# Layer 0 of a four-layer graph network: the destinations' one-hot compared with places held in PSUM

## The chip, the core and the metric

The kernel runs on one core of a Trainium2 chip. Its time is the device time of one launch in microseconds (us); smaller is better. The core's engines run unsynchronized and hand work to each other through semaphores: TensorE (PE, with its weight loads as PEld), VectorE (DVE), ScalarE (ACT), GpSimd (POOL) and SyncE (SP). Here POOL issues the indirect gathers and SP the plain DMAs.

## The reference, cut to what matters

Four layers follow each other on 6250 nodes and 100,000 edges, sorted by destination. The change is in layer 0, an attention over each node's incoming edges:

```
alpha = leaky_relu(s[src] + s[dst], 0.2)        # per edge and head
m     = segment_max(alpha, dst)
e     = exp(alpha - m[dst])
a     = e / segment_sum(e, dst)[dst]
attn  = segment_sum(Vh[src] * a, dst)           # then a projection, norms and a feed-forward
```

The edges also carry a loop from every node to itself. For each edge, `s[dst]` and the subtracted maximum have to be fetched from the destination's row, and the weighted values have to be added into the destination's row. The kernel does both with matrices of zeros and ones.

## The kernel before

**Groups.** The edges are cut into G = 98 groups of 1024 (8 columns j of 128 edges). Because the edges are sorted, a group's destinations lie in a window of 128 nodes that begins at 64*g - 32. A node block of 128 rows is put together from the windows that overlap it.

**The layer-0 edge loop** (from L812 on, under a schedule written out by hand: every engine keeps exactly the order of the source) runs once for each group g:

- POOL issues eight gathers of source rows into one of six buffers (`rows0`, L130; tile `xbuf`). A buffer may be filled again only when the sums of the group six before it are done.
- SP loads the group's destination numbers, spread over all partitions (`drow`, L742), two groups ahead, into three buffers.
- `logits0` (L771, L123, L773 on DVE) makes `al`, the exponent; ACT takes its exponential twice: into PSUM as `ex` (tile `ps_E`, L774) and into the gathered rows (L775).
- `one_hot_t` (L748 on DVE) makes `to` for the **next** group: for each edge, in the transposed layout, a one in the partition whose node is the edge's destination. It compares `drow` (int32) with a per-partition number, column g of `place`.
- L836 on DVE multiplies the gathered values by `ex`, in place.
- `of_dst` (L763 on PE) multiplies `to` of the next group with the score table, into one of two PSUM buffers `ps_A`. The next group's logits read it.
- `sum_window` (L681 on PE) sums the group's rows into `ps_S` with a second one-hot, `oh` (L754 on DVE, made a group ahead); ACT copies the sum out as `ws` (L691).
- Every second group also closes a node block: L699 (`ps_T`, shifted sums of the windows), L781 to L786 (division), L792 and L800 (turn and project), L808 and L810 (residual and statistics).

On ACT the order is: both exponentials of g, `ws` of g, in every second group the copy L794, then the exponentials of g + 1. On DVE it is: `al` of g, `to` of g + 1, the product L836 of g, then the rest. On PE it is: shifted sums or projection, `of_dst` of g + 1, the sum of g.

PSUM has eight buffers here, of which the tag "E" is one; it is taken anew for each group by `ps("E", ...)`.

Of the kernel before, what the change touches and what calls it, by code (L numbers as in the profile page):

```python
# [13 lines left out]
OP = mybir.AluOpType  # L14
# [3 lines left out]
P = 128  # L18
J = 8
W = 128  # L20
D = 256
H = 8
# [13 lines left out]
def tile_gnn(ctx: ExitStack, tc: tile.TileContext, a: dict, out: bass.AP, N: int):  # L36
# [11 lines left out]
    nc = tc.nc  # L48
# [3 lines left out]
    G = GJ // J  # L52
# [69 lines left out]
    def leaky(o, y, slope):  # L122
        nc.vector.scalar_tensor_tensor(o, y, slope, y, op0=OP.mult, op1=OP.max)  # L123
# [76 lines left out]
    with ExitStack() as l0:  # L200
        wp = l0.enter_context(tc.tile_pool(name="w0", bufs=1))
        ps = l0.enter_context(Psum("psa", T=2, Q=2, V=2, X=2))
# [453 lines left out]
    def fast():  # L656
        wp = fctx.enter_context(tc.tile_pool(name="wl", bufs=1))
        psc = fctx.enter_context(ExitStack())
        ps = psc.enter_context(Psum("ps0", S=2, A=2, T=1, B=2, E=1))
# [57 lines left out]
        with tc.tile_pool(name="e0", bufs=2) as ep:  # L717

            scw = ep.tile([P, NB, 2, 2 * H], F32, name="scw", bufs=1)
            for odd in range(2):  # L720
                for b0, b1 in ((0, 32), (32, NB)):
# [6 lines left out]
                    else:  # L728
# [5 lines left out]
            place = ep.tile([P, G], F32, name="place", bufs=1)  # L734
            nc.gpsimd.iota(place, pattern=[[HW, G]], base=-OFF, channel_multiplier=1,
                           allow_small_or_imprecise_dtypes=True)
            sums, drows, tos, dgs, ohs, mades, vs, ms, mts = {}, {}, {}, {}, {}, {}, {}, {}, {}

            def loads0(g):
# [4 lines left out]
            def one_hot_t(g):  # L744

                if g < G:
                    tos[g] = ep.tile([P, J * P], F32, name="to")
                    nc.vector.tensor_scalar(tos[g], drows[g], place[:, g:g + 1], None, OP.is_equal)  # L748

            def one_hot0(g):  # L750
                if g < G:
# [14 lines left out]
            def logits0(g):  # L766

                vg, dg = vrows[g % NV], dgs[g]
                al = ep.tile([P, J, H], F32, name="al")
                ex = ps("E", [P, J, H])  # L770
                nc.vector.tensor_tensor(al, vg[:, :, D:D + H], dg[:, :, 0:H], OP.add)  # L771
                leaky(al, al, 0.2)
                nc.vector.tensor_tensor(al, al, dg[:, :, H:2 * H], OP.subtract)  # L773
                nc.scalar.activation(ex, al, AF.Exp)  # L774
                nc.scalar.activation(vg[:, :, D:D + H], al, AF.Exp)  # L775
                return ex
# [35 lines left out]
            with tc.manual_schedule():  # L812
                for g in range(2):
                    loads0(g)
                one_hot_t(0)
                one_hot0(0)
                of_dst(0)
                for g in range(G + 2):
                    vg = vrows[g % NV]
                    if AHEAD <= g < G:  # L820
                        rows0(g)
                    loads0(g + 2)
                    for b in blocks_done(g):
                        vs[b] = ep.tile([P, H, HD], F32, name="v")
                        nc.sync.dma_start(vs[b], vt[b * P:(b + 1) * P, 0:D].rearrange("p (h c) -> p h c", c=HD))
                    if g == 6:
                        made(of1)
                    if g == 8:
                        made(of2)
                    summed = [(b, sum_block(sums, b, VR)) for b in blocks_done(g - 1)]  # L830
                    projected = [(b, project0(b)) for b in blocks_done(g - 2)]
                    if g < G:
                        ex = logits0(g)
                        one_hot_t(g + 1)
                        vals = vg[:, :, 0:D].rearrange("p j (h c) -> p j h c", c=HD)
                        made_g = nc.vector.tensor_tensor(  # L836
                            vals, vals, ex[:, :, :, None].to_broadcast([P, J, H, HD]), OP.mult)
                    of_dst(g + 1)
                    for b, s in summed:
                        attn0(b, s)  # L840
                    if g < G:
                        sums[g], summed0[g] = sum_window(ep, ohs[g], vg, VR, made_g, landed[g])
                    for b, s in summed:
                        turn0(b)
                    one_hot0(g + 1)
                    for b, t in projected:
                        residual0(b, t)
# [215 lines left out]
        ps = fctx.enter_context(Psum("ps2", S=2, A=1, T=2, B=2, C=1))  # L1063
# [397 lines left out]
    with tc.If(general < 1):  # L1461
        with ExitStack() as fctx:
            fast()
# [57 lines left out]
```

## Time and profile before

| | us |
|---|---|
| time, median of 3 runs (lowest to highest) | 5256.51 (5249.32 to 5259.04) |
| profiled execution's own time | 5219.05 |
| its span, first to last instruction | 5217.2 |
| layer-0 edge loop in it (first `al` to the last sum) | 249 to 1411 |
| busy in the whole span: PE / POOL / DVE / ACT | 3222.9 / 3037.9 / 2099.3 / 605.5 |

Busy times are sums over one engine's instructions. The engines overlap, so no busy time by itself tells the span; what decides is, at each place, the wait that ends last. In a listing of groups the columns are: line, engine, operation, output<-inputs, shapes and count, then the sum of busy time and the mean of one in ns, then the idle time of the engine just before them and what ended it. In a timeline the first number is the start, the second the duration, and the brackets hold the idle time of that engine just before and who ended it.

### The profile page before, as it was taken

What the parts mean: (1) busy time and instruction counts of PE and PEld (TensorE: products, weight loads), DVE (VectorE), ACT (ScalarE), POOL (GpSimd) and SP (SyncE); (2) the same over time, 40 slices, a digit from 0 to 9 for tenths busy, and PEclk for the clock granted to TensorE, in tenths of its full rate; (3) what the DMA queues carried; (4) which work ended last, traced back from release to release, by engine and by line L of the source; (5) the groups of instructions that cost most, each with busy time, mean ns of one, the idle gap of its engine ahead of it and who ended that gap; (6) DMA issues with size and microseconds to landing.
All of it is one profiled execution on the core that took longest, in us unless ns stands there. A gap on an engine that the chain in (4) does not pass through costs nothing. (4 is left out here: it accounts for less than half of the span.)

```text
span 5217.2 us, 42030 instructions
## 1 busy us (share of the span) xinstructions
PE 3222.9 (62%) x12132; PEld 2447.3 (47%) x12133; DVE 2099.3 (40%) x6391; ACT 605.5 (12%) x1559; POOL 3037.9 (58%) x3215
## 2 busy tenths in 40 slices
PE   7577778777896145545446466666666365555555
PEld 4356666666645134434334244554544244343344
DVE  5355555555525146566556333333323122221122
ACT  3100000000134000000000022222222000000000
POOL 0356666666302756666663466666666466666665
PEclk9777777787898567777777677777777676766677
DMA  2444444444400234344343233333333233333332
GB/s 97 119 123 141 143 139 144 140 143 140 128 0 28 82 90 114 102 112 114 104 111 102 70 100 98 98 100 98 98 97 96 69 100 99 99 98 98 99 101 83
DMA packets 258740, 536.78 MB, mean 103 GB/s; under 512 B 65096, under 2 KB 144966, under 8 KB 258502
## 3 DMA queue, kind: packets, MB, share of 16 engines
q0 software_dynamic: 137984, 364.28, 25.3%
q1 hardware_dynamic: 107750, 156.85, 9.9%
q10 hardware_dynamic: 12768, 12.85, 0.8%
q8 instruction: 105, 1.72, 0.1%
q14 instruction: 133, 1.09, 0.1%
HBM read 504.57 MB, written 29.15 MB: 102 GB/s over the span
## 5 line engine op out<-in xcount | busy, mean ns | idle before, releaser
L130 POOL DMA_INDIRECT vg<-xt,src_i x1568 | 1488.8, 950 | 890.1 <-issue 546.9
L681 PE MATMUL ps_S<-vg,oh 128*128 128x258 f32 (+1 forms) x3136 | 1023.2, 493 | 560.0 <-issue 392.9
L681 PEld LDWEIGHTS ps_S<-vg,oh 128*128 128x128 f32 x3136 | 793.3, 257 | 751.3 <-issue 439.2
L130 POOL DMA_INDIRECT xbuf<-vt,src_i x784 | 764.1, 975 | 426.2 <-issue 234.9
L130 POOL DMA_INDIRECT big<-ht,src_i x784 | 742.1, 947 | 388.3 <-issue 216.4
L699 PE MATMUL ps_T<-ws,shifts 128*128 128x265 f32 (+2 forms) x1164 | 403.0, 465 | 563.0 <-issue 264.5
L681 PE MATMUL ps_S<-oh,big 128*128 128x128 f32 x1568 | 287.8, 358 | 516.4 <-DVE big L1026 410.5
L699 PEld LDWEIGHTS ps_T<-ws,shifts 128*128 128x128 f32 x1164 | 245.2, 222 | 711.6 <-issue 340.8
L681 PEld LDWEIGHTS ps_S<-oh,big 128*128 128x128 f32 x1568 | 266.1, 264 | 547.3 <-issue 467.4
L1095 DVE TENSOR_SCALAR oh<-iota,rel,ex 128x128 f32<-128x128 f32 x784 | 210.6, 350 | 717.9 <-ACT ex L1092 483.5
L681 PE MATMUL ps_S<-xbuf,oh 128*128 128x265 f32 x1568 | 486.0, 474 | 8.3 <-issue 8.1
L681 PEld LDWEIGHTS ps_S<-xbuf,oh 128*128 128x128 f32 x1568 | 366.5, 240 | 91.9 <-issue 10.9
L1150 DVE TENSOR_SCALAR oh<-iota,rel 128x128 f32<-128x128 f32 x784 | 164.0, 298 | 550.8 <-remote 347.2
L836 DVE TENSOR_TENSOR xbuf<-xbuf,ps_E 128x2048 f32<-128x2048 f32 x98 | 223.9, 2285 | 241.4 <-issue 145.6
L763 PEld LDWEIGHTS ps_A<-scw,to 128*128 128x128 f32 x1568 | 259.9, 256 | 60.7 <-DVE to L748 45.4
L763 PE MATMUL ps_A<-scw,to 128*128 128x16 f32 x1568 | 254.6, 308 | 47.3 <-DVE to L748 45.1
L691 ACT ACTIVATE ws<-ps_S 128x265 f32<-128x265 f32 (+1 forms) x196 | 76.3, 389 | 1773.2 <-remote 623.4
L988 DVE TENSOR_SCALAR oh<-iota,rel,cut 128x128 f32<-128x128 f32 x784 | 211.6, 362 | 0.0
L980 PE MATMUL ps_A<-wr,rb 99*128 99x384 f32 (+1 forms) x588 | 194.6, 468 | 9.6 <-DMA rb<-in_rbf 9.6
L900 POOL TENSOR_TENSOR xbuf<-xbuf,bout 128x1024 f32<-128x1024 f32 (+1 forms) x13 | 29.0, 2229 | 285.5 <-ACT xn L898 278.7
L1026 DVE TENSOR_TENSOR big<-big,ps_A 128x384 f32<-128x384 f32 (+1 forms) x294 | 131.9, 504 | 85.6 <-DMA big<-ht,src_i 59.9
L754 DVE TENSOR_SCALAR oh<-iota,rel 128x128 f32<-128x128 f32 x784 | 164.2, 297 | 0.0
(226 smaller groups left out, 2935.8 us busy)
## 6 DMA issues: line engine op xcount, KB each, us to landing
drow<-in_dst_row SPq DMA_DIRECT2D x98, 512.0 KB
ea<-in_edge_attr SPq DMA_DIRECT2D x98, 512.0 KB
vg<-xt,src_i POOLq DMA_INDIRECT x1568
xbuf<-vt,src_i POOLq DMA_INDIRECT x784
big<-ht,src_i POOLq DMA_INDIRECT x784
rb<-in_rbf SPq DMA_DIRECT2D x196, 49.5 KB
vt<-row SPq DMA_DIRECT2D x49, 132.5 KB
xt<-row SPq DMA_DIRECT2D x49, 129.0 KB
```

The lines of the kernel that those rows point to most:

```text
L130: return nc.gpsimd.indirect_dma_start(out=rows, out_offset=None, in_=table, in_offset=bass.IndirectOffsetOnAxis(ap=idx[:, j:j + 1], axis=0))
L681: m = wait_for(nc.tensor.matmul(s, l, r, start=j == 0, stop=j == len(pairs) - 1), made)
L691: nc.scalar.activation(ws, s, AF.Copy)
L699: nc.tensor.matmul(t, shift_by(s), sums[g], start=i == 0, stop=i == len(parts) - 1)
L754: mades[g] = nc.vector.tensor_scalar(ohs[g][:, j, :], iota, rel[:, g * J + j:g * J + j + 1], None, OP.is_equal)
L763: nc.tensor.matmul(dgs[g][:, j, :], tos[g][:, j * P:(j + 1) * P], scw[:, g // 2, g % 2, :], start=True, stop=True)
L836: made_g = nc.vector.tensor_tensor(vals, vals, ex[:, :, :, None].to_broadcast([P, J, H, HD]), OP.mult)
L980: filtered[g] = nc.tensor.matmul(t, rbs[g][0:33 * n, g % 2, q, :], wr3[0:33 * n, 0:n, :], start=True, stop=True)
L988: nc.vector.tensor_scalar(ohs[g][:, j, :], iota, rel[:, c], w1["cut"][:, c], OP.is_equal, OP.mult)
L1026: made_g = nc.vector.tensor_tensor(hg[:, js, :], hg[:, js, :], t, OP.mult)
L1095: made_g = nc.vector.tensor_scalar(oh[:, j, :], iota, rel[:, g * J + j:g * J + j + 1], ex[:, j:j + 1], OP.is_equal, OP.mult)
L1150: made_g = nc.vector.tensor_scalar(oh[:, j, :], iota, rel[:, g * J + j:g * J + j + 1], None, OP.is_equal)
```

## The change

The destinations' places are copied once from SBUF into the PSUM buffer "E", behind the 64 columns that hold `ex`. That buffer is now taken once for the whole loop instead of once for each group. The comparison becomes an operation of two tensors, whose second input is one column of the PSUM tile, repeated over all 1024 columns.

```
             place = ep.tile([P, G], F32, name="place", bufs=1)
             nc.gpsimd.iota(place, pattern=[[HW, G]], base=-OFF, channel_multiplier=1,
                            allow_small_or_imprecise_dtypes=True)
+
+            ex_place = ps("E", [P, J * H + G])
+            exs = ex_place[:, 0:J * H].rearrange("p (j h) -> p j h", h=H)
+            nc.vector.tensor_copy(ex_place[:, J * H:], place)
...
                     tos[g] = ep.tile([P, J * P], F32, name="to")
-                    nc.vector.tensor_scalar(tos[g], drows[g], place[:, g:g + 1], None, OP.is_equal)
+                    nc.vector.tensor_tensor(tos[g], drows[g], ex_place[:, J * H + g:J * H + g + 1]
+                                            .to_broadcast([P, J * P]), OP.is_equal)
...
                 al = ep.tile([P, J, H], F32, name="al")
-                ex = ps("E", [P, J, H])
+                ex = exs
```

The instructions keep their order on every engine; one copy is added on DVE ahead of the loop. The waits written into the built program differ in one kind: each comparison in the loop now also waits for ACT, for the exponential into PSUM of the current group (L774), because that writes the tile which the comparison reads. In exchange the product L836 no longer carries that wait: it comes behind the comparison on DVE.

## The prediction

> **What bounds the loop now.** I read the windows view first, because only the layer-0 loop is touched (columns: us, then busy us of PE, PEld, DVE, ACT, POOL, then TensorE clock, DMA share, GB/s).
>
> ```profile
> 249.00:1411.00 1162.00, 910.40 (x4007) 758.74 (x4008) 622.90 (x1713) 92.06 (x344) 717.88 (x736) 0.79 0.47 139
> ```
>
> DVE, whose work grows, is busy 54% of the loop, PE 78%, POOL 62%: no engine is full. So the loop is a chain handed from engine to engine; the waits view for 250 to 1400 us says where.
>
> ```profile
> ACT ws L691 <- remote: 454.1, 38, 17.0
> ...
> DVE al L771 <- remote: 151.4, 24, 10.6
> DVE xbuf L836 <- issue: 145.6, 33, 5.4
> ...
> PE ps_T L699 <- ACT ws L691: 112.6, 29, 9.8
> ```
>
> ACT waits for sums, PE waits for the copy of the sum, DVE waits in front of the product L836. The timeline shows the pattern, which repeats every two groups: 49 pairs in 1162 us, 23.7 us each.
>
> ```profile
> 805.65 0.77 DVE L748 TENSOR_SCALAR to<-drow,place 128x1024 f32<-128x1024 int32 x1
> ...
> 810.30 0.24 ACT L774 ACTIVATE ps_E<-al 128x64 f32<-128x64 f32 x1
> ...
> 810.57 2.29 DVE L836 TENSOR_TENSOR xbuf<-xbuf,ps_E 128x2048 f32<-128x2048 f32 x1 [4.15 <-issue]
> ...
> 811.46 1.86 PE L763 MATMUL ps_A<-scw,to 128*128 128x16 f32 x16
> ...
> 813.17 3.83 PE L681 MATMUL ps_S<-xbuf,oh 128*128 128x265 f32 x16
> ...
> 822.29 0.22 DVE L771 TENSOR_TENSOR al<-xbuf,ps_A 128x64 f32<-128x64 f32 x1 [6.64 <-remote]
> 822.45 0.39 ACT L691 ACTIVATE ws<-ps_S 128x265 f32<-128x265 f32 x1 [11.56 <-remote]
> ...
> 822.80 0.22 DVE L773 TENSOR_TENSOR al<-al,ps_A 128x64 f32<-128x64 f32 x1
> ...
> 822.94 0.75 DVE L748 TENSOR_SCALAR to<-drow,place 128x1024 f32<-128x1024 int32 x1
> 823.12 0.23 ACT L774 ACTIVATE ps_E<-al 128x64 f32<-128x64 f32 x1 [0.28 <-DVE al L773]
> 823.16 1.35 POOL L130 DMA_INDIRECT xbuf<-vt,src_i  x1 [2.98 <-ACT ws L691]
> ...
> 823.60 2.28 DVE L836 TENSOR_TENSOR xbuf<-xbuf,ps_E 128x2048 f32<-128x2048 f32 x1
> ```
>
> Two halves are to be seen. In the **tight half** (from 822.3) the logits, the comparison `to` and the product follow each other without a gap. The exponential (ends 823.35) runs beside `to` (ends 823.69), so the product does not wait for it. PE's `of_dst` of the next group starts at 823.94 behind `to`, takes 3.46 us at a granted clock of about 0.5, and the sum runs 827.25 to 833.51; `ws` follows at 833.54, at once. All this is on the path. In the **loose half** (from 805.65) `to` is made early and DVE then idles 4.15 us, because ACT does `ws` before the exponential. After the product PE is quick (clock 1.0: 1.86 and 3.83 us, sum recorded as ended at 817.0), but `ws` starts only at 822.45. These 5.4 us are a delay that the trace puts down to nothing ("remote"). In this stretch POOL issues the second batch of eight gathers, 810.47 to 820.18.
>
> **Part 1, the longer operation.** `to` falls from tensor-scalar to two tensors, one in PSUM. The trace has no int32 comparison with PSUM; the nearest row is an elementwise operation of 1024 columns with a repeated PSUM input (first row: now; second: the neighbour).
>
> ```profile
> L748 DVE TENSOR_SCALAR to<-drow,place 128x1024 f32<-128x1024 int32 x98 | 76.3, 778 | 10.9 <-POOL place L735 10.9
> L1031 DVE TENSOR_TENSOR ea<-ea,ps_K 128x1024 f32<-128x1024 f32 x98 | 119.0, 1214 | 0.0
> ```
>
> The product L836 says the same: 2285 ns for 2048 columns, half of it and a little of fixed cost is about 1.2. I take 1.21 us; against the 0.748 us of an undisturbed `to` that is +0.466 us. Over 98 groups: 45.7 us more DVE time. From below, the row could be 0.75 (no loss of rate); from above, I see no reason for more than 1.3.
>
> **Part 2, the added wait.** `to` of g+1 now waits for the exponential of g. Behind it on DVE stands the product of g, and for `to` waits `of_dst` on PE, which stands ahead of the sum of g. The wait takes `to` out of the exponential's shadow.
>
> - Tight half: `to` can start when the product now could by the exponential, 823.35 + 0.06 (from the exponential's end at 810.54 to the product at 810.57 there is 0.03; 0.06 allows for an overlap of 0.06 that L748 and L836 show) = 823.41 instead of 822.94. It ends at 824.6 instead of 823.69: +0.47 wait, +0.47 length, together +0.9. The product starts 0.9 later; `of_dst` 0.8 later, since PE's shifted sums (until 824.15) held it a little. The sum of g: **+0.84** (0.8 to 0.9).
> - Loose half: `to` moves from 805.65 to 810.57, so the product starts 1.12 later and `of_dst` 0.46 later; the sum +0.9. This lies beside the 5.4 us between the sum's recorded end and `ws`. If that delay has its own cause, nothing of this is paid; if it is a fixed latency, all is.
>
> I went through the 98 groups of the trace with this rule. 51 have no such delay behind the sum: 8 pay under 0.1 us, 11 about 0.46 (5.0), 28 between 0.6 and 0.97 (23.6), 4 at the start over 1 (6.4); together **+35.3 us**. The other groups are covered; uncovered they would add 39.6, **+75 us** in all.
>
> **Part 3, what goes.** The product loses its own wait for ACT: worth nothing, as it stands behind `to` on DVE, which has it now. `ex` is one buffer as before (tag "E" has one), so no overlap between groups is lost: the exponential of g+1 waited for the product of g and still does. Gathers: the first gather of the batch at 823.16 takes 1.35 us beside `to` against 0.945 otherwise. 131 of some 744 gathers overlap `to`; they take 1.093 us on average, those with no overlap 0.947, together 19.4 us. Here a rule of the Trainium skill speaks for the change: page "SBUF — State Buffer", section "Who interferes with whom": VectorE and GpSimd share one pair of ports under an exclusive lock; the section's reading of a tensor-scalar operation between SBUF tensors is that GpSimd is shut out to its end[...]. By the rule one gather a pair is held 799.48 to 800.01, 0.53 us x 49 = 26 us (an estimate from the page); by the rows 0.40 us x 49 = 19.4. In the tight half the batch ends some 0.5 us before `ws` releases the next, so neither figure is on the path; I count 0, and keep 20 us for a rival.
>
> A second rule bears on the same place: "TensorE: Matmul & The Clock Gate", section "Why this matters for your kernels", wants no PE gaps above about 3 us, or the clock falls to half. The row shows it: a gap of 4.46 us at 822.89, and then the windows
>
> ```profile
> 809.00:822.00 13.00, 8.90 (x52) 7.30 (x50) 5.01 (x13) 1.05 (x4) 8.30 (x9) 1.00 0.48 143
> 822.00:833.00 11.00, 10.11 (x33) 8.45 (x34) 7.59 (x22) 0.88 (x3) 7.71 (x8) 0.54 0.51 157
> ```
>
> If the loose half's sum moves into the delay, the gap shrinks by 0.9 to 3.5 us. By the rule that is close to staying warm, and `of_dst` and the sum of the tight half would fall from 9.6 to 5.7 us. By the rows it isn't: gaps of 2.5 us (489 us) and 3.7 us (1095 us) were followed by a clock of 0.5 all the same. And where a pair did stay warm, its length was still 23.3 to 25.1 us. I count 0.
>
> **Part 4, ahead of the loop.** One copy of 98 columns to PSUM, some 0.2 us. It waits for `place` (221.85 us), and DVE's copies behind it now wait too, so the first `of_dst` comes about 2 us later; the first logits wait for gathers until 249.02, 20 us of cover. Nothing. The loads of `drow` are freed later by at most 1 us, with some 20 us in hand. After the loop the layers are the same code.
>
> **Sum.** 0 + 35.3 + 0 + 0 = +35 us on the profiled execution, 5219 to 5254. That execution is 37 us under the median shown; on the median's scale 5256.5 + 35 = **5291 us**, +0.7%.
>
> **Rivals.**
>
> 1. *The period is held by something else, and the tight half's delay vanishes in the loose one.* For it: pairs whose tight half already ran longer had the same sum (23.63 to 23.66 us), since `ws` came 1.4 to 2.0 us behind the gathers' end instead of 2.0 to 2.8; the clock's switches stand on a grid of 3.41 us and seven of these, 23.9, are close to a pair. Against: the second batch starts 0.71 us behind `ws`, so a late `ws` shifts everything that I can name. It gives 0 to +10 us: 5257 to 5267. Chance 0.17.
> 2. *The delay behind the loose sum is a fixed latency*: every group pays, +75: 5332. Against: it varies between pairs, and is near zero where pairs are warm. Chance 0.13.
> 3. *Faster, by POOL.* The two batches take 9.7 to 10.3 us each, with 0.71, 0.3 and about 2.5 us of hand-over 23.7: if the end of the gathers is what releases `ws` in both halves, the pair lasts as long as POOL's chain, and 0.40 us less for the first gather decides. Price 19.4 us: 5237. It wins only if the batch's slack in the tight half (0.5 us before, 1.3 or more after) is not real, that is, if the sum waits for the gathers' end. Chance 0.14.
> 4. *The comparison with PSUM costs no more than now* (0.75 us): only the wait is left, +0.47 of 0.9 in the tight half, half of 35: 5274. It counts to my forecast's side; it and its variants up to +50 have the rest, 0.56.
>
> **Range and chances.** A measurement here tells 0.2%, 10.5 us, from no change. Faster 0.14 (rival 3), within it 0.18 (rival 1 and the lowest of rival 4), slower 0.68. The range reaches from a part of rival 3 to rival 2: 5243 to 5335. The forecast's own: 5274 to 5305.
>
> **What would show it.** `to` at 1.2 us and 98 of them, starting just behind L774 in all groups; the product straight behind `to`; in the tight half `ws` to `ws` 0.8 us longer (11.1 to 11.9) and in the loose half unchanged (12.7); first gathers at 0.95. A loose half that gives the 0.8 us back shows rival 1; one that grows by 0.9, rival 2; a pair below 23.5 us, rival 3. I am wrong altogether if the loop's length changes by less than 15 us or `to` takes under 1 us.

## The result, and the profile after

| | before | changed |
|---|---|---|
| time, median of 10 runs (us) | 5256.09 (5249.32 to 5262.59) | 5272.99 (5264.28 to 5284.07) |
| ratio | | 1.0031 (1.0022 to 1.0040) |
| span of the profiled execution | 5217.2 | 5263.5 |
| in it, first `al` to the last product | 1158.1 | 1181.6 |

The change costs 16 us (ratio 1.0031 of 5256; 12 to 21 by the interval). The forecast was +35: the right side, a size of twice too much. The two spans differ by 46 us, 23.5 of them in the layer-0 loop; nearly all of the rest is in later stages, whose code is the same: from the last product to the end, before took 3810 us and after 3834. The profiled execution of before lay 37 us under its kernel's median, that of after 8 us under. So the spans alone would mislead here, and the length of the loop too; the ten runs decide.

Two groups of the page of before, in the columns of the page (busy us and mean ns, then the idle time before and what ended it):

```profile
L130 POOL DMA_INDIRECT xbuf<-vt,src_i x784 | 764.1, 975 | 426.2 <-issue 234.9
...
L836 DVE TENSOR_TENSOR xbuf<-xbuf,ps_E 128x2048 f32<-128x2048 f32 x98 | 223.9, 2285 | 241.4 <-issue 145.6
```

And of after:

```profile
L130 POOL DMA_INDIRECT xbuf<-vt,src_i x784 | 748.1, 954 | 457.8 <-issue 202.8
...
L752 DVE TENSOR_TENSOR to<-drow,ps_E 128x1024 f32<-128x1024 int32 x98 | 119.7, 1221 | 372.5 <-ACT ps_E L779 270.9
L841 DVE TENSOR_TENSOR xbuf<-xbuf,ps_E 128x2048 f32<-128x2048 f32 x98 | 223.5, 2280 | 2.6 <-ACT ps_E L779 2.6
```

The comparison takes 1221 ns (1.21 was taken), DVE now idles 372 us in front of it instead of 241 in front of the product, and the product follows it without a wait: part 1 and the path of part 2 as foretold. The gathers fell from 764.1 to 748.1 us of POOL time, 16 us where part 3 had 19.4.

The waits of after for 250 to 1400 us (engine, line, waited for, us in total, times, longest):

```profile
ACT ws L691 <- PE ps_S L681: 396.4, 36, 11.8
ACT ws L691 <- remote: 365.8, 32, 16.6
DVE to L752 <- ACT ps_E L779: 264.1, 71, 5.5
...
DVE al L776 <- remote: 49.0, 12, 10.4
...
PE ps_T L699 <- ACT ws L691: 24.8, 17, 6.8
```

Before, `al` waited 151.4 us for "remote" and PE 112.6 us for `ws`; now 49.0 and 24.8. So waits went that the forecast had left standing. ("Remote" means little here: of one DMA semaphore, which counts gathers, the trace of before holds 2028 events, that of e4 below 6270, so many waits have lost their releaser.) The timeline of one pair of after shows how:

```profile
1146.66 0.39 ACT L691 ACTIVATE ws<-ps_S 128x265 f32<-128x265 f32 x1 [11.44 <-PE ps_S L681]
1146.95 0.22 ACT L779 ACTIVATE ps_E<-al 128x64 f32<-128x64 f32 x1
1147.20 1.22 DVE L752 TENSOR_TENSOR to<-drow,ps_E 128x1024 f32<-128x1024 int32 x1 [5.13 <-ACT ps_E L779]
...
1148.34 2.28 DVE L841 TENSOR_TENSOR xbuf<-xbuf,ps_E 128x2048 f32<-128x2048 f32 x1
...
1150.72 3.83 PE L681 MATMUL ps_S<-xbuf,oh 128*128 128x265 f32 x16 [0.22 <-issue]
...
1158.85 0.39 ACT L691 ACTIVATE ws<-ps_S 128x265 f32<-128x265 f32 x1 [11.51 <-remote]
1159.41 0.23 ACT L779 ACTIVATE ps_E<-al 128x64 f32<-128x64 f32 x1
...
1159.67 1.22 DVE L752 TENSOR_TENSOR to<-drow,ps_E 128x1024 f32<-128x1024 int32 x1 [5.51 <-ACT ps_E L779]
1160.81 2.28 DVE L841 TENSOR_TENSOR xbuf<-xbuf,ps_E 128x2048 f32<-128x2048 f32 x1
...
1164.71 6.30 PE L681 MATMUL ps_S<-xbuf,oh 128*128 128x265 f32 x16
...
1171.05 0.39 ACT L691 ACTIVATE ws<-ps_S 128x265 f32<-128x265 f32 x1 [11.24 <-PE ps_S L681]
```

In both halves now the comparison comes behind the exponential (5 us of DVE idle ahead of it), so neither half is tight. The halves of this pair are 12.19 and 12.20 us from `ws` to `ws`. Over 80 groups (12 to 91) the half that was tight, the odd groups, went from 11.07 to 11.64 us on average and the loose one, the even groups, from 12.77 to 12.47. The time that passes between a sum's recorded end and `ws`, called the late report from here on, is still there in one half (sum recorded as ended at 1154.55, `ws` at 1158.85), but in the one that used to be tight. I split the way from one `ws` to the next at the start and at the recorded end of the sum's matmuls, for the same 80 groups of each trace; means per group in us, the late report without the 0.04 us that every sum takes:

| trace | `ws` to `ws` | `ws` to sum's start | sum's start to `ws` | of it, the sum | of it, late report |
|---|---|---|---|---|---|
| before | 11.92 | 4.25 | 7.67 | 5.07 | 2.56 |
| changed | 12.05 | 4.87 | 7.18 | 5.48 | 1.66 |

The sum starts 0.62 us later on average. It also takes 0.41 us longer, as the TensorE clock granted during the sums fell from 0.81 to 0.72. So its end comes 1.03 us later, but the late report is 0.90 us shorter. What is left is 0.13 us a group, 13 us over 98.

The late report goes with the clock: before, 40 of the 80 sums ran at a granted clock of 0.97 or more, and theirs is 4.93 us, against 0.19 for the others; after, 15 did, with 4.06 us, against 1.1. The profile models the ends of matmuls, so it can't tell a late report from a sum that runs on beyond its recorded end.

### The profile page after: what moved, and what is told of

The parts are those of the page before. It is cut to its first block, busy times and chain, and to the rows that moved or that the text cites. A ratio compares the mean times of both kernels' runs of the same rounds, so it can differ in the third digit from the quotient of the medians.

```text
span 5263.5 us, 42128 instructions
## 1 busy us (share of the span) xinstructions
PE 3243.2 (62%) x12132; PEld 2467.9 (47%) x12133; DVE 2144.8 (41%) x6392; ACT 605.7 (12%) x1559; POOL 3027.3 (58%) x3215
## 4 chain that ended last, share of the span: by engine, by line
PE 37%; issue 16%; another core or an unknown queue 16%; DVE 15%; POOL 10%; ACT 3%; DMA 1%; DVEq 0%; ACTq 0%; POOLq 0%; SPq 0%
PE ps_S L681 21%; POOL vg L130 8%; DVE oh L993 3%; PE ps_A L768 3%; DVE oh L1100 2%; DVE big L1031 2%; PE ps_T L699 2%; PE ps_A L452 2%; PE ps_B L458 2%; POOL big L130 2%; PE ps_Q L256 2%; DVE to L752 1%; PE ps_C L1129 1%; PE ps_C L1046 1%
## 5 line engine op out<-in xcount | busy, mean ns | idle before, releaser
L681 PE MATMUL ps_S<-vg,oh 128*128 128x258 f32 (+1 forms) x3136 | 998.4, 483 | 633.2 <-issue 321.6
L681 PEld LDWEIGHTS ps_S<-vg,oh 128*128 128x128 f32 x3136 | 774.4, 251 | 828.3 <-issue 379.8
L130 POOL DMA_INDIRECT xbuf<-vt,src_i x784 | 748.1, 954 | 457.8 <-issue 202.8
L699 PE MATMUL ps_T<-ws,shifts 128*128 128x265 f32 (+2 forms) x1164 | 361.7, 442 | 412.6 <-issue 264.7
L681 PE MATMUL ps_S<-oh,big 128*128 128x128 f32 x1568 | 300.3, 370 | 512.0 <-DVE big L1031 392.5
L681 PE MATMUL ps_S<-xbuf,oh 128*128 128x265 f32 x1568 | 532.8, 510 | 13.4 <-issue 13.2
L681 PEld LDWEIGHTS ps_S<-oh,big 128*128 128x128 f32 x1568 | 278.1, 275 | 543.1 <-issue 461.2
L681 PEld LDWEIGHTS ps_S<-xbuf,oh 128*128 128x128 f32 x1568 | 399.1, 261 | 112.6 <-issue 16.2
L1155 DVE TENSOR_SCALAR oh<-iota,rel 128x128 f32<-128x128 f32 x784 | 162.6, 294 | 539.2 <-remote 395.7
L752 DVE TENSOR_TENSOR to<-drow,ps_E 128x1024 f32<-128x1024 int32 x98 | 119.7, 1221 | 372.5 <-ACT ps_E L779 270.9
```

Source lines behind the costliest of these rows:

```text
L130: return nc.gpsimd.indirect_dma_start(out=rows, out_offset=None, in_=table, in_offset=bass.IndirectOffsetOnAxis(ap=idx[:, j:j + 1], axis=0))
L681: m = wait_for(nc.tensor.matmul(s, l, r, start=j == 0, stop=j == len(pairs) - 1), made)
L699: nc.tensor.matmul(t, shift_by(s), sums[g], start=i == 0, stop=i == len(parts) - 1)
L752: nc.vector.tensor_tensor(tos[g], drows[g], ex_place[:, J * H + g:J * H + g + 1] .to_broadcast([P, J * P]), OP.is_equal)
L1155: made_g = nc.vector.tensor_scalar(oh[:, j, :], iota, rel[:, g * J + j:g * J + j + 1], None, OP.is_equal)
```

## The experiments

The kernel before takes 4500 us on some chips, 5212 to 5256 on others; the same kernels were run on both kinds. The first ten runs fell on the quicker kind, the next six on one chip of the slower kind (that of the result was of this kind too), the last two on the quicker again. Each run is compared with the kernel before on its own chip.

### The quicker kind: the parts of the change one by one

e1, the longer operation alone, both inputs in SBUF (run again as e7 and e10):

```
-nc.vector.tensor_scalar(tos[g], drows[g], place[:, g:g + 1], None, OP.is_equal)
+nc.vector.tensor_tensor(tos[g], drows[g], place[:, g:g + 1].to_broadcast([P, J * P]), OP.is_equal)
```

> Kernel before, with the comparison as an operation of two tensors that both lie in SBUF: the longer operation without the wait for ACT. Theory A (my sum, with its size too large because only part of each delay is paid: the changed kernel took +17 us where its own delays sum to +35): the comparison takes about 1.2 us, stays in the exponential's shadow, product 0.47 us later in the tight half; +8 us if about half is paid, +17 us if all is. Theory B (all of the delay is paid, and shorter gathers give 16 to 19 us back): +17 us if the gathers beside the comparison still take 1.1 us on average, about 0 if they fall to 0.95. Theory C (the loop's period is fixed by something else, and the +17 us come from elsewhere): 0 us in the loop.

e2, the wait alone, the short operation reading its number from the shared PSUM tile (again as e6):

```
-nc.vector.tensor_tensor(tos[g], drows[g], ex_place[:, J * H + g:J * H + g + 1]
-                        .to_broadcast([P, J * P]), OP.is_equal)
+nc.vector.tensor_scalar(tos[g], drows[g], ex_place[:, J * H + g:J * H + g + 1], None, OP.is_equal)
```

> Changed kernel, with tensor-scalar again, its number read from the PSUM tile: the wait for ACT with the short comparison (0.75 to 0.8 us). Theory A: +8 us (half of my 0.47 us in the tight half), +17 at most. Theory B: the comparison still lengthens the gathers (1.1 us on average where they overlap), so nothing is given back: +17 us or more. Theory C: as the changed kernel, since the pattern of the loop is set by the wait.

e3, the comparison of the changed kernel twice in a row:

```
+for _ in range(2):
     nc.vector.tensor_tensor(tos[g], drows[g], ex_place[:, J * H + g:J * H + g + 1]
```

> Changed kernel, with the comparison made twice in a row: 1.22 us more on DVE between the exponential and the product in every group. If the tight halves alone pay it in full: 45 x 1.22 = +55 us over the changed kernel, +72 over before. If about half of each delay is paid: +27, +44 over before. If every group pays: +119, +136 over before. Theory C: under +20 over the changed kernel.

e4, the kernel before for another trace:

> Kernel before, unchanged, for a second trace. If the first trace is typical: the layer-0 loop takes 1162 us within 3 us and the whole span is near 5217 us. If the first trace was a lucky execution: the span is 30 us or more longer, and where it is longer says which stage varies from one execution to the next.

Measured: e1 4542.55 against 4503.29 us, ratio 1.0090 (1.0077 to 1.0104), +39 us; e2 0.9965 (0.9951 to 0.9978), **18 us faster**; e3 1.0322 (1.0308 to 1.0336), +144; e4 4504.24. None of the three theories has that pattern. The trace of e4 says why: this chip shows another kernel. Two groups of it, in the columns of the groups:

```profile
L130 POOL DMA_INDIRECT xbuf<-vt,src_i x784 | 785.0, 1001 | 241.3 <-issue 211.3 <-DVE al L773 22.5 <-DMA vt<-row 2.9
...
L771 DVE TENSOR_TENSOR al<-xbuf,ps_A 128x64 f32<-128x64 f32 x98 | 21.6, 220 | 317.6 <-DMA xbuf<-vt,src_i 227.3 <-PE ps_S L681 57.7 <-PE ps_T L699 29.6
```

The logits wait 227 us for gathers. In no group of 12 to 91 is a sum reported late, though 27 of them ran at full clock. The ring of six buffers runs empty by about group 18, after which `al` mostly starts 2 us behind its own last gather. In the two traces of the result `al` starts 42 us or more behind its gathers: there the ring is always full. So on the quicker kind POOL bounds the loop of before, and what the comparison does to a gather beside it is what counts:

| kernel | mean of gathers beside / not beside the comparison (us) | extra POOL time | loop (us) |
|---|---|---|---|
| before (e4) | 1.290 / 0.955 | 36 | 985.9 |
| length alone (e1) | 1.546 / 0.954 | 72 | 1021.5 |
| wait alone (e2) | 1.085 / 0.952 | 17 | 962.1 |
| changed (e5) | 0.946 / 0.956 | -2 | 960.2 |

From before to e1 the gathers cost 36 us more and the loop 36; from before to e2 it is 19 less and 24 less. With two inputs in SBUF the operation holds the gather longer than tensor-scalar did. With one in PSUM it holds it not at all, which is the form that the change has. e3 is another case: its `al` stays 41 us or more behind its gathers, so its ring is full, and the way through DVE and PE sets its group (5.50 us to the sum and 5.83 of sum make nearly all of 11.37).

The changed kernel beside e2 and e1 once more:

> The changed kernel once more, to anchor the runs beside it, since the kernel before took 4503 us on the chip of the first four runs and 5256 on the chip of the result. On a chip like that of the result: +17 us again. On a chip like that of the first four runs, where the loop's length moved with the time of the gathers (1.29 us beside the comparison, 0.955 otherwise, 36 us together): -36 us from the gathers, less what the wait costs; the wait alone cost nothing there, so -15 to -36 us.

> The wait with the short comparison. On a chip like that of the result: theory A (a part of each delay is paid) +8 us; theory B (the tight halves pay in full, the gathers give back 19 us in the changed kernel) +17 us, as the gathers stay at about 1.09 us beside the comparison here. On a chip like that of the first four runs: -18 us again.

> The longer comparison without the wait, both inputs in SBUF; beside it a gather took 1.55 us in the first call. On a chip like that of the result: theory A +8 us, as the gathers are not on the path; theory B, where gathers count in full, +17 for the length and 72 - 19 = 53 for the gathers, +50 to +70 us. On a chip like that of the first four runs: +39 us again.

e5 0.9952 (0.9939 to 0.9966): on this kind the change makes the kernel **faster, by 22 us**. Its gathers, with the mean back at 954 ns:

```profile
L130 POOL DMA_INDIRECT xbuf<-vt,src_i x784 | 747.8, 954 | 255.1 <-issue 212.5 <-ACT xbuf L780 13.6 <-DVE al L778 11.3
```

e6 0.9963 (0.9949 to 0.9977) and e7 1.0093 (1.0077 to 1.0108) repeat e2 and e1.

e8 gives the places a PSUM tile of their own, so that no wait is needed; e9 also makes the comparison two groups ahead, behind the product:

```
-        ps = psc.enter_context(Psum("ps0", S=2, A=2, T=1, B=2, E=1))
+        ps = psc.enter_context(Psum("ps0", S=2, A=2, T=1, B=1, E=1, L=1))
...
+            ps_place = ps("L", [P, G])
+            nc.vector.tensor_copy(ps_place, place)
```

> The changed kernel with the places in a PSUM tile of their own, so that the comparison does not wait for ACT (tag B gives up one of its two buffers for it). The operation is the same 1.22 us. On chips like those of the first two calls (before 4500 us, changed 4478): the gathers are freed (about -36 us) and the wait is gone, so at least as fast as the changed kernel, -22 to -36 us against before; if the wait was what made the loop faster there (wait alone gave -16 us), it is slower than the changed kernel. On a chip like that of the result (before 5256, changed +17): theory A +8 us; theory B, gathers count in full, +17 for the length less 19, about -2 us.

> As the one before, and the comparison made two groups ahead and behind the product, so that neither the product nor TensorE's fetch of the destinations' rows waits for it. If the comparison's place on the path is what costs: faster than the one before by 5 to 40 us on either kind of chip. If POOL's gathers bound the loop once they are freed: the same as the one before within 5 us.

> The longer comparison with both inputs in SBUF, beside the own tile: the same length, no wait in either, only the gathers differ (1.55 to 1.66 us beside this one). On chips like those of the first two calls: +40 us against before again. On a chip like that of the result: theory A, as the own tile, +8; theory B, 70 us over the own tile.

e8 0.9932 (0.9919 to 0.9946), -30 us; e9 0.9934 (0.9921 to 0.9948), the same; e10 1.0084 (1.0068 to 1.0099). The wait costs the changed kernel some 8 us here; with it gone the gathers bound the loop (944.9 us), and where the comparison stands no longer matters. e8 and e9 beat the kernel before on this kind and, in separate sets of runs, the changed one by some 8 us.

### The slower kind: the case itself

> Sent for the chip more than for the kernel: all calls so far fell on chips where the kernel before takes 4500 us. There it is +40 us once more. On a chip like that of the result (5256): theory A (a part of each delay is given back by TensorE, whatever the gathers do) +8 to +17 us; theory B (the gathers' time counts in full) +50 to +70 us.

> Own tile, no wait, beside the one before: the same length, freed gathers. On the chips so far: -30 us again. On a chip like that of the result: theory A +8 to +17 us, as the length alone; theory B about -2 us.

Before 5212.04 us. e11 ratio 1.0006 (0.9998 to 1.0015), +4 us at 5216.16; e12 1.0025 (1.0016 to 1.0033), +13. The gathers of e11:

```profile
L130 POOL DMA_INDIRECT xbuf<-vt,src_i x784 | 795.0, 1014 | 400.2 <-issue 211.1 <-ACT xbuf L775 75.5 <-ACT mt L794 47.1
```

They take 31 us more than before (795.0 against 764.1; 1.291 us beside the comparison), and the loop took 1159.0 us against 1158.1: **theory B falls** for this kernel. What a gather takes is not felt in it. That freeing the gathers gave nothing back in the changed kernel too is inferred from this; no run makes its gathers longer on this kind. But my +17 for the length is not there either. Four more runs on the same chip:

e13, the kernel before with the own tile's single buffer in tag B (`B=2` to `B=1`, nothing else), and e14 to e16, the kernels of e2, e3 and e5:

> The kernel before with one buffer instead of two in the PSUM tag B, the control of the own tile. If the missing buffer is free, as the turn and the projection alternate: 0 us within 5 on either kind of chip, and the own tile's +13 us on the slower kind is of the freed gathers or of chance. If it costs: +5 to +13 on the slower kind.

> The wait with the short comparison. On the slower kind: if the wait is what the changed kernel pays, +10 to +17 us; if wait and length add up only together, 0 to +6; by my own sum, half of 35, +17. On the quicker kind -16 us again.

> The changed kernel with the comparison made twice, 1.22 us more in every group, 119 us in all. On the slower kind: if about 30% of a delay reaches the time, as the changed kernel's trace says, +36 us over the changed kernel; if the tight halves alone pay in full, +55; if all pay, +119. On the quicker kind +165 over the changed kernel again.

> The changed kernel as the anchor on the same chip. On the slower kind +17 us against before, on the quicker -22.

Before 5252.25 us, 40 us more than in the runs just above, on the same chip and with the same code. The traces show two levels too: from the last product to the end they take 3807 to 3810 us (before, e11, e12) or 3832 to 3836 (after, e13 to e16). So only what ran together is compared. Against 5252.25:

| kernel | ratio (95% interval) | us |
|---|---|---|
| e13, one B buffer | 1.0012 (1.0003 to 1.0020) | +8 |
| e14, wait alone | 1.0004 (0.9995 to 1.0013) | +3 |
| e16, changed | 1.0031 (1.0020 to 1.0041) | +17 |
| e15, comparison twice | 1.0069 (1.0056 to 1.0083) | +39 |

So e12's +13 is in good part the missing buffer. Wait alone (+3) and length alone (+4) can't be told from nothing; together they cost 17. And 1.22 us more in each group, 119 us in all, cost 22: a share of 0.19. The gathers are the same in both (0.945 us beside the comparison), so they can't have given the rest back. The same step on the quicker kind (e5 to e3, in two sets of runs) cost 165. That is more than 119, since the granted clock in the loop fell from 0.85 to 0.80 and the sums got longer.

The split of the path, as above, shows where the other four fifths stay. e13 stands for the kernel before, of which there is no trace at the higher level:

| trace | `ws` to `ws` | `ws` to sum's start | sum's start to `ws` | of it, the sum | of it, late report |
|---|---|---|---|---|---|
| e11, length alone | 11.96 | 4.38 | 7.58 | 5.08 | 2.47 |
| e13, one B buffer | 12.02 | 4.21 | 7.81 | 5.17 | 2.61 |
| e14, wait alone | 12.09 | 4.44 | 7.65 | 5.23 | 2.38 |
| e16, changed | 12.13 | 4.87 | 7.26 | 5.53 | 1.69 |
| e15, twice | 12.30 | 5.92 | 6.38 | 5.75 | 0.60 |
| e3, twice, quicker kind | 11.37 | 5.50 | 5.87 | 5.83 | 0 |

From e13 to e16 the sum's end comes 1.02 us later, the late report is 0.92 shorter, and 0.11 us a group is left, 11 us in the loop, where the times differ by 9. In e15 the sum ends 2.35 us later than in the trace of before, and the late report has shrunk by 1.96; 0.38 us a group is left, 37 us in the loop, and 39 were timed. One trace is one execution, though: e14's has almost the length of e16's, while its kernel is timed at +3. The timed costs are 16 of 101 us of delay at the sum's end (the change) and 39 of 230 (e15): about a sixth is paid. A stretch of e15's timeline:

```profile
967.39 0.39 ACT L691 ACTIVATE ws<-ps_S 128x265 f32<-128x265 f32 x1 [11.41 <-PE ps_S L681]
...
967.94 2.48 DVE L753 TENSOR_TENSOR to<-drow,ps_E 128x1024 f32<-128x1024 int32 x2 [3.85 <-ACT ps_E L780]
968.10 0.94 POOL L130 DMA_INDIRECT xbuf<-vt,src_i  x1 [2.63 <-ACT xbuf L781]
...
970.33 2.28 DVE L842 TENSOR_TENSOR xbuf<-xbuf,ps_E 128x2048 f32<-128x2048 f32 x1
...
970.56 2.18 PE L769 MATMUL ps_A<-scw,to 128*128 128x16 f32 x16 [1.41 <-DVE to L753]
...
972.71 5.19 PE L681 MATMUL ps_S<-xbuf,oh 128*128 128x265 f32 x16
...
976.88 0.95 POOL L130 DMA_INDIRECT xbuf<-vt,src_i  x1 [0.31 <-issue]
...
979.59 0.39 ACT L691 ACTIVATE ws<-ps_S 128x265 f32<-128x265 f32 x1 [11.51 <-PE ps_B L798]
```

From `ws` to `ws` 12.20 us, with both comparisons on the path. Of 72 groups (20 to 91) 50 lie between 12.05 and 12.30 us here, 32 and 47 in the changed kernel's two traces, 4 in that of before, and 6 to 21 in those of e11 to e14: the more delay is put in, the more groups sit near this length.

### What holds a group at 12 us

> Kernel before, whose layer-0 sums take only the first four of a group's eight columns, so half of that matmul work is left out of the computation. On the slower kind: if TensorE's late sums hold the group at 12 us, the loop gets shorter by 2 to 3 us a group, 200 to 300 us; if POOL's batch does, by under 30 us. On the quicker kind, where POOL bounds the loop: under 30 us.

> Kernel before with a ninth gather in each group from the seventh on (column 0 again), 1.25 us more of POOL. On the slower kind: if POOL's batch holds the group at 12 us, +115 us (92 groups); if it runs beside something longer, under 40 us, and 0 if 0.9 us of slack a group covers most of it. On the quicker kind +115 us.

e17, the kernel before with half of the sums' matmuls left out, and e18, the kernel before with a ninth gather in each group:

```
-            end = sum_tiles(s, [(oh[:, j, :], rows[:, j, :]) for j in range(J)], made, got)
+            end = sum_tiles(s, [(oh[:, j, :], rows[:, j, :])
+                                for j in range(J // 2 if n == VR else J)], made, got)
```

```
-                     for j in range(J)]
+                     for j in ([*range(J)] if g < NV else [*range(J), 0])]
```

Both fell on the quicker kind (before 4500.55): e17 0.9995 (0.9986 to 1.0004), e18 1.0226 (1.0209 to 1.0243), +103 us. They confirm that POOL bounds the loop of before there: half of the sums' matmuls gone brings nothing, and a batch that is 1.04 us longer in the trace (11.20 against 10.16 in e4; 96 us over 92 groups) is felt in full. For the slower kind they say nothing.

The traces of the slower kind do say something. POOL's next batch of eight gathers refills the buffer whose sum has just been reported, and starts 0.71 us behind `ws` (median of each trace below). Means of the batch, and the time from its end to the next `ws` (median, and a tenth of the groups below and above), in us:

| trace | batch | batch's end to `ws` |
|---|---|---|
| before | 9.98 | 1.38 (-0.35 to 2.65) |
| e11, length alone | 10.31 | 0.41 (-2.37 to 2.55) |
| changed | 9.78 | 1.73 (0.38 to 2.40) |
| e15, twice | 9.76 | 1.76 (1.70 to 1.98) |
| e3, twice, quicker kind | 9.76 | 0.48 (0.31 to 1.97) |

In e15 the three pieces, 0.71 + 9.76 + 1.76, make 12.2 us, the length at which the groups sit. There `ws` starts as the batch's eighth gather reports its landing (in the stretch above from 979.50 on, with `ws` at 979.59), also where the sum had been recorded as ended earlier (by 1.3 us in the median of the 39 groups with a late report). So in the changed kernels the sum's report keeps step with POOL's batch. Whether it waits for the batch is not shown. Before and in e11 at least a tenth of the `ws` come ahead of the batch's end, and e11's batch is 0.33 us longer with the group no longer. What holds a group at 12.2 us therefore stays open. A ninth gather in the changed kernel, on a chip of the slower kind, would tell.

## Why the prediction was off

- **Part 1, the operation at 1.21 us: right** (1221 ns; DVE 45.5 us more in the page).
- **Part 2, the path: right.** The comparison waits for the exponential in every group, and product, `of_dst` and sum move with it. The sum's start moves by 0.62 us on average; the group by group rule had 35.3 + 39.6 us over 98 groups, 0.76.
- **Part 2, who pays: wrong; this is the step that failed.** "51 have no such delay behind the sum" and pay 35.3 us, "the other groups are covered". I took the late report for a property of the groups that had it in one trace. It is not: with the sum moved, it shrinks in one half and appears in the other (even groups 4.32 to 1.03 us, odd 0.80 to 2.29), so the cover is for all groups, and a delay anywhere is paid in part. The tight half grew by 0.57 us where 0.8 was foretold, and the loose one, to be unchanged, gave 0.30 back. The term of 35.3 us was 16.
- **Part 3, the clock at 0: wrong where it matters, without a cost of its own that can be told apart.** The mean of the windows view of 249 to 1411 us hardly moved (0.78 after, 0.79 before), but the clock during the sums fell from 0.81 to 0.72, and each sum took 0.41 us longer, 40 us in all. This delay lies ahead of the late report as well, so the two are paid together: 16 us of 101. Of the two gaps that I set against the rule cited there, the one of 3.7 us is longer than the rule allows and so agrees with it; only the one of 2.5 us speaks against it.
- **Part 3, freed gathers at 0: in keeping with what was tried on this kind of chip**: e11 made them 31 us longer and cost 4. It was not tried in the changed kernel, whose groups keep step with the batch. The Trainium skill, page "SBUF — State Buffer", section "Who interferes with whom", says that a VectorE operation with at most one SBUF input, outside the modes that use both pairs of ports, does not contend with GpSimd; the changed comparison is of this form, and the trace agrees: a gather beside it takes 0.947 us. With both inputs in SBUF (e1) a gather beside it took 1.55 us.
- **Rival 1** ("the tight half's delay vanishes in the loose one") had the mechanism, with a size of 0 to +10 for 16 measured; I gave it 0.17. The evidence that I set against it, a second batch of gathers that starts behind `ws`, is there in all traces of this kind, but e11 shows that a longer batch need not lengthen the group. **Rival 2** (all pay, +75) is out. **Rival 3** (faster, by POOL, 19 us) is false here and true on the quicker kind, where the change gave -22.

## What to carry to other kernels

A gap behind an operation that the trace can't put down to anything is slack with no owner: price a delay in front of it between nothing and full for every iteration, not full where the gap is missing and nothing where it stands. Read the clock where the matmuls are that matter, not as a mean over the loop. Whether a ring of buffers runs empty (how short a time a tile's first reader comes behind its load) tells whether the loop waits for its producer's data; ask that of each chip that the kernel is to run on, since the same change was +0.31% on one kind and -0.48% on the other.

## What was unexpected of the hardware

- Chips differ in kind: the same program took 4500 us on three and 5212 to 5256 elsewhere, with a mean granted TensorE clock of 0.82 against 0.76. Why is not known, and one chip of the slower kind took 5212 and, soon after, 5252. The late reports of the sums (2.56 us a group) are in the traces of the slower kind alone.
- An int32 comparison of 1024 columns takes as long with its second input in PSUM (1221 ns) as in SBUF (1217 to 1221); the form decides whether gathers beside it are held: tensor-scalar 1.06 to 1.29 us, both inputs in SBUF 1.29 to 1.66, one in PSUM 0.95, not beside it 0.95.
